# Layer 1's first product in groups of four samples, with two levels of Strassen's method

## The chip, the cores and the metric

The kernel runs on one core of a Trainium2 chip, as one launch. The metric is the time of that launch on the device in microseconds (us), the median of several executions. A profile of one execution shows where the time goes. The engines are named as the profile names them: PE is TensorE (matmuls; PEld is its loading of weights), DVE is VectorE, ACT is ScalarE, POOL is GpSimd, SP is SyncE, which here only issues DMA transfers.

## The reference

Four graph layers work on a batch of 128 samples, each with 128 nodes of 512 features; every layer ends in a residual sum and a layer norm. The change is in layer 1, a hypergraph convolution with a hidden width of 1024:

```
H  = (adj != 0);  w = adj's first row                  # 128 x 128 per sample
Dn = 1 / (H w);   Be = 1 / (column sums of H)          # guarded against 0
conv(x, W, b) = Dn * (H (Be * (H^T (x W^T)))) + b

h = relu(conv(x, W1, b1))       # 512 -> 1024
h = layer_norm(h, gamma, beta)
y = conv(h, W2, b2)             # 1024 -> 512
x = layernorm(x + (y + x))
```

Layer 0 is a graph diffusion with three weight matrices, layer 2 an attention over a product of adjacency and exp(tanh), layer 3 an eight-head attention with the adjacency as mask. All is in fp32.

## The kernel before, in words

**A recorded plan.** The kernel doesn't issue instructions as its Python runs. The names `pe`, `ve`, `ac`, `po` and `sp` are recorders: each call adds an operation with its tiles and with the current `plan.key`, a number that says when the operation should come (one unit is one pair of samples). At the end `Plan.emit` (line 356) orders all operations with a list scheduler that has a cost for each operation and a latency between engines, and issues them. That is why nearly all instructions carry line 367 of `emit`: one tells them apart by engine, operation and tile. Every engine then works through its own queue in that fixed order.

**Tiles.** SBUF tiles have kinds with a fixed number of places: `four` (1024 columns, 12 places, and more that come from other kinds once those are no longer needed), `sq` (pairs of 128x128), `col` (small columns), `out` (layer 0's results), `k` (the small matrices K). The big tile `first` holds layer 0's weights (kind `w7`) at first; later the same space holds layer 1's second weights (`w28`) and layer 3's query and key weights (`q7`). The dictionary `later` says which places come free when which others are done. PSUM has eight banks: six of kind `bank` and two (`t0`, `t1`) that layer 0 uses for itself and that are banks later.

**Strassen's method.** A product of a pair of samples (two blocks of 128 rows) with a weight matrix is done with seven products instead of eight. `strassen` (line 549) issues them in three banks: in bank `al` four products accumulate one after the other, and between two of them the sum so far is read out, so each waits for the eviction before it. `take` is a dictionary of evictions, by name of the result. `operands` makes the four sums of the left side on POOL. With `twice`, the method is used at two levels on two pairs of samples: seven calls of `strassen`, one for each of the outer products, 49 inner products in all, of one matmul each. Outer sums of the left side come from `lefts`, and two additions per half join the outer results. Layer 0's product and layer 3's query and key product use `twice` already.

**Layer 1 before** (`layer1`, called for each of 64 pairs of samples) has eight stages with the keys of `WHEN1`: load x1 and the adjacency; turn it, make H and the scaled H; make K = H Be H^T and Dn; multiply x1 with K (YT) and form `operands`, and also make q, which holds 2 x + b2 and the term of beta; the first product with W1; the turning of h by way of DRAM; the second product with W2; the product with K, layer norm, store. The first product is one-level Strassen with two matmuls of 512 columns in each of the seven products. Each eviction on DVE scales by Dn and adds b1 on its way out of PSUM:

```
return lambda p: ve.scalar_tensor_tensor(d, p, scale[u], b, op0=OP.mult, op1=OP.add)
```

When a quarter of the result is complete, `then` runs relu on ACT on its 512 columns, takes its statistics on DVE, and after a sample's second half normalizes the sample.

**The order of the layers.** The last lines start `layer0`, `layer1` and `layer23` one after the other in keys, with `LAG1` and `LAG2` as distance, so that a layer's first groups overlap with the last of the layer before. `prepare1`, `prepare2`, `prepare_w` and `prepare3` load and combine the weights of later layers while an earlier layer runs.

Of the kernel before, what the change touches and what calls it, by code (L numbers as in the profile page):

```python
# [13 lines left out]
AF = mybir.ActivationFunctionType  # L14
# [3 lines left out]
P = 128  # L18
# [19 lines left out]
WHEN1 = (-3.0, -2.3, -1.25, -.8, 0, 1.0, 1.4, 2.0)  # L38
WHEN2 = (-2.4, -2.0, -1.45, -1.15, -.7, .3, .5, 2)
WHENV, WHENS, WHENP, WHENO = (.9, 1.9), (2.2, 3.2), (3, 4), (3.5, 4.5)  # L40
LAG1, LAG2 = 1, -.25
# [22 lines left out]
SIZE = {"four": U * D, "sq": U * (P + 2), "bank": D, "col": 12, "row": D, "w28": 7168, "q7": 7 * 2 * P,  # L64
# [311 lines left out]
def kernel(  # L376
# [19 lines left out]
    for kind, n, at in (("w7", 7, 0), ("q7", 7, 0), ("w28", 1, 7 * SIZE["q7"])):  # L396
        places[kind] = [first[:, at + k * SIZE[kind]:at + (k + 1) * SIZE[kind]] for k in range(n)]
        if kind != "w7":
            for k in range(n):
                lo, hi = at + k * SIZE[kind], at + (k + 1) * SIZE[kind] - 1  # L400
                later[kind, k] = [("w7", i) for i in range(lo // SIZE["w7"], min(hi // SIZE["w7"], 6) + 1)]
    slots = {"w7": 7, "out": OUTS, "q7": 0, "w28": 0, "sq": SQS, "col": COLS, "row": ROWS, "bank": 6, "t0": 1, "t1": 1,
# [35 lines left out]
    def four():  # L438

        return tile_of("four", U, D)  # L440
# [25 lines left out]
    class Seven:  # L466
# [5 lines left out]
        def __getitem__(self, key):  # L472
            return self.tiles[key[1]][(key[0], *key[2:])]

# [482 lines left out]
    def prepare1():  # L957
# [4 lines left out]
        WT["w1"] = Seven([four().rearrange("p c f -> p c f") for _ in range(7)])  # L962
        yield from load_T(WT["w1"], [w1], 2, D)
        gb = four().rearrange("p u f -> p (u f)")
# [15 lines left out]

    def layer1(i0):
        x1 = load_rows(x1d[i0 // U])
        ab = from_dram(adj[i0:i0 + U], sq)
        yield
        AT = sq()
        turned(AT, ab)
        HT = sq()
        cnt = col(U)
        for b in range(U):
            ve.tensor_scalar(HT[:, b], AT[:, b], 0.0, None, op0=OP.not_equal, op1=OP.add,  # L990
                                    accum_out=cnt[:, b:b + 1])
        po.tensor_scalar(cnt, cnt, 1.0, None, op0=OP.max)
        po.tensor_tensor(cnt, cnt, minus1, OP.pow)
        M = P + 2
        HB = sq(M)
        for b in range(U):
            po.tensor_scalar(HB[:, b, :P], HT[:, b], cnt[:, b:b + 1], None, op0=OP.mult)
        po.tensor_copy(HB[:, :, P:P + 1], AT[:, :, 0:1])
        po.memset(HB[:, :, P + 1:P + 2], 1.0)
        yield  # L1000
        pk = bank()
        with plan.together():
            for b in range(U):
                pe.matmul(pk[:, b * M:(b + 1) * M], HT[:, b], HB[:, b], start=True, stop=True)
        K = tile_of("k", U, M)
        ac.copy(K.rearrange("p b n -> p (b n)"), pk[:, :U * M])
        Dn = col(U)
        dsafe = col(U)
        deg = pk[:, :U * M].rearrange("p (b n) -> p b n", n=M)[:, :, P]
        ve.tensor_scalar(dsafe, deg, 1.2e-38, None, op0=OP.max)  # L1010
        ve.reciprocal(dsafe, dsafe)
        ve.scalar_tensor_tensor(Dn, deg, 0.0, dsafe, op0=OP.is_gt, op1=OP.mult)
        drd = col(U)
        po.tensor_tensor(drd, Dn, K[:, :, P + 1], OP.mult)
        yield
        YT = four().rearrange("p u (c n) -> p u c n", n=P)
        for b in range(U):
            pt = bank()
            with plan.together():
                for c in range(C):  # L1020
                    pe.matmul(pt[:, c * P:(c + 1) * P], x1[:, b, c * P:(c + 1) * P], K[:, b, :P],
                              start=True, stop=True)
            ac.copy(YT[:, b].rearrange("p c n -> p (c n)"), pt)
        ops = operands(*blocks(YT))

        q = four()
        for b in range(U):
            po.tensor_tensor(x1[:, b], x1[:, b], b2h, OP.add)
            ac.mul(q[:, b], bw2, drd[:, b:b + 1])
            ve.scalar_tensor_tensor(q[:, b], x1[:, b], 2.0, q[:, b], op0=OP.mult, op1=OP.add)  # L1030
        yield
        h = [four() for _ in range(U)]
        dn = [Dn[:, b:b + 1] for b in range(U)]
        take = biased_take((h[0][:, 0], h[0][:, 1], h[1][:, 0], h[1][:, 1]),
                           b1_b * 2, dn)
        sts = [col(12) for _ in range(U)]
        left = [2, 2]

        def then(f, b, g):
            def run(p):  # L1040
                t = h[b][:, g]
                f(p)
                ac.activation(t, t, AF.Relu)
                stats(sts[b], g, t)
                left[b] -= 1
                if not left[b]:
                    nmr, rstd = norm_terms(sts[b], 2)
                    ac.activation(h[b], h[b], AF.Identity, bias=nmr, scale=rstd)
            return run

        for k, b, g in (("c11", 0, 0), ("c12", 0, 1), ("c21", 1, 0), ("c22", 1, 1)):
            take[k] = then(take[k], b, g)
        strassen(ops, WT["w1"], 2, D, take)
# [297 lines left out]
```

## Time and profile before

| | before |
|---|---|
| time, median of 3 | 5501.85 us (5497.74 to 5502.41) |
| span in the profile | 5492.0 us |
| instructions | 88697 |
| DMA, mean share of 16 engines | 131 GB/s moved |
| layer 0 | about 0 to 1300 us |
| layer 1 | about 1350 to 3160 us |
| layers 2 and 3 | about 3200 us to the end |

The layers are told apart by the forms of their matmuls: 386 columns in layer 0, 512 and 256 in layer 1, 256 and 128 after it. In the page's timeline each digit is the busy share of a fortieth of the span, in tenths:

```profile
PE   8999999999999999999999999999999999999998
DVE  6787887877676666666666678777777777777776
ACT  2333333334333333333333334444444444444444
POOL 6777777766666666666666578888888888888887
```

DVE and POOL are the least busy in the stretch from the eleventh to the twenty-third digit, which is layer 1.

### The profile page before, as it was taken

The numbers are of one execution on the slowest core, as the hardware profiler recorded it, in microseconds if no ns is written. First come the engines' busy times: TensorE is split into PE (matmuls) and PEld (weight loads), VectorE is DVE, ScalarE is ACT, GpSimd is POOL, SyncE is SP. The second block draws the span as 40 slices with busy tenths as digits, with TensorE's granted clock in tenths as the row PEclk, the third lists the DMA queues.
The fourth block names the chain that finished last, engine by engine and source line by source line (L and its number), as shares of the span: only waits on it lengthen the run. The fifth ranks groups of instructions, "written<-read, shape, count | busy, mean of one in ns | idle before, by whom it ended". The sixth has DMA issues, their size and how long they took to land.

```text
span 5492.0 us, 88697 instructions
## 1 busy us (share of the span) xinstructions
PE 5408.3 (98%) x27801; PEld 4003.2 (73%) x27801; DVE 4015.5 (73%) x9010; ACT 2255.4 (41%) x5839; POOL 3993.5 (73%) x5848
## 2 busy tenths in 40 slices
PE   8999999999999999999999999999999999999998
PEld 4555555554666666666666788989999998999987
DVE  6787887877676666666666678777777777777776
ACT  2333333334333333333333334444444444444444
POOL 6777777766666666666666578888888888888887
PEclk9999999999999999999999999999999999999999
DMA  3333333333444444333444445555555555555543
GB/s 89 111 94 105 93 98 104 95 106 120 134 130 120 120 116 116 114 115 115 120 120 120 132 122 155 166 159 161 162 158 157 164 154 158 166 162 155 160 151 128
DMA packets 752508, 717.39 MB, mean 131 GB/s; under 512 B 261787, under 2 KB 573091, under 8 KB 752038
## 3 DMA queue, kind: packets, MB, share of 16 engines
q1 hardware_dynamic: 750534, 709.11, 43.3%
q8 instruction: 221, 3.62, 0.3%
q10 hardware_dynamic: 1504, 2.62, 0.2%
q14 instruction: 249, 2.04, 0.1%
HBM read 393.76 MB, written 317.72 MB: 130 GB/s over the span
## 4 chain that ended last, share of the span: by engine, by line
PE 87%; DVE 4%; DMA 3%; POOL 2%; issue 2%; ACT 1%; SPq 1%; DVEq 0%; POOLq 0%; ACTq 0%
PE bank L367 66%; PE t L367 20%; DVE out L367 2%; SPq L367 1%; DVE col L367 1%; DMA out<-h 1%; DVE four L367 1%; ACT out L367 1%; POOL col L367 0%; POOL out L367 0%; POOL four L367 0%; DVE first L367 0%; DVE sq L367 0%; DMA four<-in_x_dram 0%; POOL first L367 0%
## 5 line engine op out<-in xcount | busy, mean ns | idle before, releaser
L367 DVE TENSOR_TENSOR out<-bank,out 128x386 f32<-128x386 f32 (+1 forms) x1949 | 951.1, 506 | 524.8 <-PE bank L367 444.0
L367 PE MATMUL bank<-first,four 128*128 128x386 f32 (+3 forms) x4416 | 1292.8, 446 | 25.4 <-DVE out L367 10.1
L367 PEld LDWEIGHTS bank<-first,four 128*128 128x128 f32 (+2 forms) x4416 | 744.5, 189 | 550.8 <-DVE out L367 129.2
L367 PE MATMUL bank<-four,out 128*128 128x256 f32 (+2 forms) x2100 | 707.7, 474 | 0.3 <-DVE four L367 0.2
L367 POOL TENSOR_TENSOR out<-out 128x256 f32<-128x256 f32 (+3 forms) x424 | 492.8, 1173 | 253.3 <-DVE out L367 202.7
L367 PEld LDWEIGHTS bank<-four,out 128*128 128x128 f32 (+1 forms) x2100 | 375.9, 190 | 253.4 <-issue 208.3
L367 ACT COPY out<-bank 128x258 f32<-128x258 f32 (+2 forms) x581 | 243.3, 421 | 627.9 <-PE bank L367 495.1
L367 PE MATMUL bank<-first,out 128*128 128x256 f32 (+3 forms) x2168 | 469.2, 372 | 1.6 <-DVE out L367 1.1
L367 POOL TENSOR_SCALAR col<-col 128x1 f32<-128x1 f32 (+1 forms) x704 | 174.5, 251 | 383.6 <-DVE col L367 357.9
L367 PEld LDWEIGHTS bank<-first,out 128*128 128x128 f32 (+2 forms) x2168 | 387.1, 188 | 56.2 <-DVE out L367 3.0
L367 POOL TENSOR_TENSOR col<-col,neghalf 128x1 f32<-128x1 f32 x640 | 392.7, 617 | 18.3
L367 ACT ACTIVATE out<-out,col,col 128x512 f32<-128x512 f32 (+1 forms) x260 | 231.8, 898 | 394.3 <-POOL col L367 385.3
L367 ACT ACTIVATE four<-four,col,col 128x512 f32<-128x512 f32 (+1 forms) x294 | 268.6, 922 | 281.6 <-POOL col L367 250.3
L367 DVE TENSOR_TENSOR four<-bank,four 128x256 f32<-128x256 f32 x573 | 236.2, 418 | 176.6 <-PE bank L367 167.0
L367 PE MATMUL bank<-out,first 128*128 128x128 f32 (+3 forms) x2192 | 344.9, 298 | 1.8 <-DVE out L367 0.7
L367 PE MATMUL bank<-four,first 128*128 128x128 f32 (+3 forms) x1612 | 317.3, 331 | 1.8 <-DVE out L367 1.5
L367 PEld LDWEIGHTS bank<-out,first 128*128 128x128 f32 (+2 forms) x2192 | 290.2, 186 | 27.6 <-issue 3.1
L367 POOL TENSOR_TENSOR four<-four,four 128x256 f32<-128x256 f32 (+2 forms) x369 | 305.1, 830 | 6.0 <-PE bank L367 1.1
L367 DVE BATCH_NORM_STATS2 col<-four 128x6 f32<-128x512 f32 x370 | 252.4, 684 | 49.9 <-ACT four L367 48.0
L367 PE MATMUL bank<-first 128*128 128x128 f32 (+1 forms) x2036 | 285.5, 278 | 3.1 <-DVE out L367 1.9
L367 PEld LDWEIGHTS bank<-first 128*128 128x128 f32 (+1 forms) x2036 | 257.5, 188 | 17.6 <-DVE out L367 2.6
L367 PEld LDWEIGHTS bank<-four,first 128*128 128x128 f32 (+2 forms) x1612 | 246.5, 189 | 28.4 <-issue 2.3
(431 smaller groups left out, 12130.4 us busy)
## 6 DMA issues: line engine op xcount, KB each, us to landing
out<-h SPq DMA_DIRECT2D x96, 512.0 KB, 4.4
h<-four SPq DMA_DIRECT2D x304, 128.0 KB, 2.4
four<-in_x_dram SPq DMA_DIRECT2D x512, 64.0 KB, 2.0
four<-in_x_dram SPq DMA_DIRECT2D x62, 512.0 KB, 3.8
x1d<-four SPq DMA_DIRECT2D x62, 512.0 KB, 2.8
out<-S SPq DMA_DIRECT2D x54, 512.0 KB, 4.3
h<-out SPq DMA_DIRECT2D x208, 128.0 KB, 2.4
S<-out SPq DMA_DIRECT2D x49, 512.0 KB, 3.1
```

The lines of the kernel that those rows point to most:

```text
L367: call(*map(real, args), **{n: real(a) for n, a in kw.items()})
```

## The change

Layer 1 now works on groups of four samples (two pairs, index r), as layer 0 and layers 2 and 3 do. Its first product goes through `lefts` and `twice`. The bias and the scale differ by column and by row, and inside the two-level scheme a partial result belongs to several outputs, so they can't be added in the eviction any more: the evictions become plain (ACT copies and DVE adds), and scale, bias and relu follow as operations on the whole row of 1024 columns.

```
 def prepare1():
-        WT["w1"] = Seven([four().rearrange("p c f -> p c f") for _ in range(7)])
+        WT["w1"] = Seven([four() for _ in range(7)])
         yield from load_T(WT["w1"], [w1], 2, D)
+        for k, j in enumerate((B11, B21, T2, T1, B22, T3, N4)):
+            yield
+            WT["w1"].tiles[j] = Split(WT["w1"].tiles[j], tile_of("q3", 3, 2 * P))
+            combine(WT["w1"].tiles[j], (ve, po)[k % 2])
...
 def layer1(i0):
...
-        take = biased_take((h[0][:, 0], h[0][:, 1], h[1][:, 0], h[1][:, 1]),
-                           b1_b * 2, dn)
...
-        strassen(ops, WT["w1"], 2, D, take)
...
+        left = lefts(YTs)
+        yield
+        base = plan.key
+
+        h = [[tile_of("h" if i0 + 2 * U < B else "four", U, D) for _ in range(U)] for _ in range(2)]
+        twice(left, WT["w1"], 2 * P,
+              lambda r, half: [h[r][b][:, half, m * 2 * P:(m + 1) * 2 * P] for b in range(U) for m in range(2)],
+              lambda r, half: [h[r][b][:, half] for b in range(U)], [lambda d: plain_take(*d)] * 2, STEP1)
+        loads = []
+        for r, i in enumerate(both):
+            plan.key = base + STEP1 * (5, 7)[r]
+            for b in range(U):
+                t = h[r][b].rearrange("p g f -> p (g f)")
+                ve.scalar_tensor_tensor(t, t, dns[r][b], rows1[:, :2].rearrange("p g f -> p (g f)"),
+                                        op0=OP.mult, op1=OP.add)
                 ac.activation(t, t, AF.Relu)
+                sts = col(12)
+                for g in range(2):
+                    stats(sts, g, h[r][b][:, g])
+                nmr, rstd = norm_terms(sts, 2)
+                ac.activation(t, t, AF.Identity, bias=nmr, scale=rstd)
```

Around it:

- The second-level parts of W1 (new kind `q3`) and the tiles of h (new kind `h`, seven places) lie in the space of layer 0's weights. The query and key weights of layer 3 (`q7`) now wait for `q3` and `h` to be done, so `prepare2` moves from the first half of layer 1 to its end, and `prepare_w` and `prepare3` move later too.
- x1 and K aren't kept in SBUF through a group: K is stored to DRAM and loaded again, and x1 is loaded a second time, before the last stage. q is made there.
- The keys of layer 1's stages are new (`WHEN1`, `STEP1` = 0.22 for the step between the seven outer products, `WHENH`, `WHENW`, `WHENG`), and `LAG2`, the distance to layers 2 and 3, goes from -0.25 to 1.5.

## The prediction

> **What bounds the kernel now.** I read the engines' shares first, then the chain that ended last, then the busy time by stage, and last the order of time inside one stage.
>
> ```profile
> PE 5408.3 (98%) x27801; PEld 4003.2 (73%) x27801; DVE 4015.5 (73%) x9010; ACT 2255.4 (41%) x5839; POOL 3993.5 (73%) x5848
> PE 87%; DVE 4%; DMA 3%; POOL 2%; issue 2%; ACT 1%; SPq 1%; DVEq 0%; POOLq 0%; ACTq 0%
> ```
>
> TensorE is busy 98% of the span and holds 87% of the chain. Four windows follow: the passage from layer 0 to layer 1, the middle of layer 1, the passage to layers 2 and 3, and these two layers.
>
> ```profile
> 1235.70:1373.00 137.30, 124.34 (x408) 64.94 (x407) 109.10 (x248) 58.03 (x125) 83.01 (x127) 0.99 0.40 120
> 1700.00:2980.80 1280.80, 1278.38 (x4929) 863.94 (x4929) 781.03 (x1544) 481.57 (x775) 788.02 (x1322) 1.00 0.40 117
> 3157.90:3295.20 137.30, 130.10 (x864) 115.84 (x863) 105.03 (x244) 53.01 (x167) 100.02 (x135) 0.99 0.41 122
> 3295.20:5354.70 2059.50, 2051.72 (x15200) 1864.77 (x15199) 1622.72 (x3882) 947.83 (x3212) 1729.44 (x2423) 1.00 0.52 159
> ```
>
> The columns after the length are PE, PEld, DVE, ACT, POOL. In layer 1 PE is busy 99.8%, DVE 61%, POOL 62%. In layers 2 and 3 PE stays at 99.6% with DVE at 79% and POOL at 84%: that is how full the helpers may be without PE noticing. The two passages lose 13.0 and 7.2 us. So time comes only from less PE work, as long as the other engines keep up.
>
> Now the order of time on PE, start and length first:
>
> ```profile
> 2000.12 3.60 PE L367 MATMUL bank<-four,out 128*128 128x512 f32 x8
> 2003.55 1.88 PE L367 MATMUL bank<-out,out 128*128 128x512 f32 x4
> 2012.21 1.89 PE L367 MATMUL t<-first,four 128*128 128x256 f32 x8
> 2013.94 1.89 PE L367 MATMUL bank<-first,four 128*128 128x256 f32 x8
> ```
>
> Each matmul leaves two records (layer 1 has 54 matmuls a pair of samples, 108 records; 4929 records are 45.6 pairs, 28.05 us each). From start to start, eight records of 512 columns take 3.43 us, so one matmul takes 857 ns; eight of 256 take 1.73 us, so one takes 432 ns.
>
> Last, the engines that share work around it:
>
> ```profile
> 2011.79 2.02 DVE L367 SCALAR_TENSOR_TENSOR out<-four,out 128x512 f32<-128x512 f32 x2
> 2011.39 1.27 POOL L367 TENSOR_TENSOR four<-four,rows 128x512 f32<-128x512 f32 x1
> 2012.62 1.02 POOL L367 TENSOR_TENSOR col<-col,neghalf 128x1 f32<-128x1 f32 x1
> 2014.54 0.55 POOL L367 TENSOR_TENSOR col<-col,neghalf 128x1 f32<-128x1 f32 x1
> ```
>
> Two DVE operations with two SBUF tensors take 2.02 us beside a POOL operation, and the small POOL operation after it takes 1.02 instead of 0.55 us.
>
> Prices by form, over the whole span (the number before the last bar is the mean of one in ns):
>
> ```profile
> L367 DVE TENSOR_TENSOR four<-bank,four 128x256 f32<-128x256 f32 x573 | 236.2, 418 | 176.6 <-PE bank L367 167.0 <-POOL four L367 2.4 <-issue 0.4
> L367 DVE TENSOR_TENSOR first<-first 128x256 f32<-128x256 f32 x16 | 8.1, 539 | 0.0
> L367 DVE TENSOR_TENSOR four<-four,four 128x1024 f32<-128x1024 f32 x6 | 7.3, 1216 | 0.0
> L367 POOL TENSOR_TENSOR four<-four,four 128x256 f32<-128x256 f32 x202 | 147.6, 731 | 4.1 <-PE bank L367 0.5
> L367 POOL TENSOR_TENSOR four<-four,four 128x512 f32<-128x512 f32 x101 | 128.3, 1272 | 0.8 <-PE bank L367 0.7
> L367 POOL TENSOR_TENSOR four<-four,four 128x128 f32<-128x128 f32 x66 | 30.1, 456 | 1.2
> ```
>
> [...] the first of the two STTs seems to wait until the POOL add ends at 2012.66, and POOL then gives time back. [...] The row of six above agrees (1216 ns); no row has 1024 columns and a scalar, and I take the same. [...] So I price PE by starts, and these agree that PE is full.
>
> **The change, part by part.** Counts are from the two built programs.
>
> 1. *The product itself.* Per four samples, 28 matmuls of 512 columns (7 products, 2 accumulations, 2 pairs) become 49 of 256. In all 896 x 0.857 = 768 us go and 1568 x 0.432 = 677 us come: **PE -91 us**, 2.84 us a group of four. The group's 56.1 us becomes 53.3 us of PE work. Weight loads rise with the matmuls, but one is 190 ns beside 432 ns and stays under it, as in the second product today.
>
> 2. *VectorE.* A group has 2 x 781.03/45.6 = 34.2 us today. It loses 14 evictions with scale (722 to 743 ns, -10.3 us) and gains 41 evictions of 256 columns (418 ns by the row, 380 ns by starts where three stand together): +15.6 to 17.1 us. It also gains four scale-and-bias operations of 1024 columns on two SBUF tensors: 1.22 us each alone, up to 2.1 if they double as the 512-column pair does (1.0 each): +4.9 to 8.4 us. Sum 44.4 to 49.4, or 83 to 93% of 53.3. I take 47. The eviction is also a wait: four products accumulate in one bank in turn, and each waits until the one before is read, so an eviction behind a 1.2 us transpose on VectorE's queue delays PE unless other products are ready. The second product (24 us a group) is such filler.
>
> 3. *GpSimd.* Today 2 x 788.02/45.6 = 34.5 us a group. Added are eight adds of 512 (four for sums of inputs, four that join the partial results; 1.272 us), four more of 256 (0.73) and four of 128 (0.456): 10.2 + 2.9 + 1.8 = +14.9 us. That is 49.4 us, 93% of 53.3. [...] 4 x 1.22 = 4.9 us if each stops an add, 4 x 0.47 = 1.9 if each meets a small operation as in the lines above. So 51.3 to 54.3 us, **96 to 102% of PE's work**; I take 52. This is the narrow place. Behind GpSimd's queue stand the sums that the next products read, so a late GpSimd stops PE.
>
> 4. *ScalarE.* Relu on 1024 columns, once a sample instead of twice on 512, and eight more copies of 256 (372 ns): about 21.1 + 2 = 23 us a group, hidden under PE.
>
> 5. *DMA.* 64 stores and 64 reloads of K (133 KB), 64 second loads of x1 (512 KB): about 50 MB on 717 MB, with the DMA share at 0.40 in layer 1. Hidden.
>
> 6. *Passage into layer 1.* The first weights get their second level: 16 VectorE subtractions (539 ns) and 12 on GpSimd (0.73 us), 8.6 and 8.8 us, beside layer 0's last products. The results lie where layer 0's weights were, so they can't be made earlier. Then the first group has 21 us of short products and no second product as filler, with 17 us of evictions. From 13 us lost I expect 23: +10.
>
> 7. *Passage out.* The query and key weights now need the space of h and of the second-level parts, so their load, turning and combining come after layer 1's last first product instead of beside layer 1. The combining alone is 16 x 0.54 + 4 x 2.33 = 18 us of VectorE. Layer 1's last second products (24 us of PE) and layer 2's first products stand beside it; the later start of layer 2 makes that room. From 7 us lost I expect 15: +8.
>
> Sum for PE's idle time inside layer 1: at 93 to 98% GpSimd I expect 1.5% of a group lost, 0.8 us, 26 us in 32 groups. Bounds: 0.2 us (as full as layers 2 and 3) and 3 us. Total: -91 + 26 + 10 + 8 = -47, **5455 us**.
>
> **The rivals.**
>
> *A (0.50), the forecast:* most of PE's saving stays, some is lost on a nearly full GpSimd. 5455.
>
> *B (0.27), all hidden:* [...] the adds fit in the gaps, the passages cost half: -91 + 6 + 9 = -76, 5426. For it: PE at 99.6% in layers 2 and 3 with the same two-level scheme. Against it: GpSimd is at 84% there, not at 93% or more.
>
> *C (0.13)[...]:* a group takes the 54.3 us of item 3 and about 1 us that its order can't fill, 55.3: -26 + 18 = -8, 5494. For it: POOL's waits on VectorE's statistics are 360 us in the layer 1 window, and a chain of three small operations leaves gaps of 0.1 us. Against it: those waits are mostly slack today.
>
> *D (0.10), slower:* GpSimd full and VectorE at 93% wait for each other, so PE's products arrive late in both: 56.5 us a group, +13, with the passages' 18: 5533. For it: each new VectorE operation waits for a GpSimd add and then stops one. Against it: they are four a group, and the products have six to eight banks.
>
> **How the numbers follow.** A is the likeliest, so the time is 5455. A and B are faster. C spreads over the border: 0.05 faster, 0.08 the same. D is slower. So faster 0.82, same 0.08, slower 0.10. For the range I take B's lower side (nothing lost in layer 1, passages +3: 5415) and C's upper side (5510); D is left out and little else.
>
> **What would show it.** Right: in the middle of layer 1, PE starts of 432 ns in the first product, POOL at 9 tenths, DVE at 8, PE at 97 to 99%, a group at about 54 us; PE waits on POOL's four and out tiles, which it hardly has today; the new 1024-column operation at 1.2 to 2.1 us. Wrong: PE below 96% in layer 1 (C or D), or a passage that loses more than 30 us; a POOL share under 88% would mean I priced its adds too high, and B would be the case.

## The result, and the profile after

The changed kernel takes 5531.85 us (5523.80 to 5539.37), beside 5502.13 us for the kernel before on the same chip: a ratio of 1.0055, 95% interval 1.0038 to 1.0073. It is slower by 30 us (0.55%) where 47 us less were forecast, and outside the range. The page of the changed kernel, engines' shares and then the chain that ended last:

```profile
PE 5368.3 (97%) x29145; PEld 4254.2 (77%) x29145; DVE 4386.7 (79%) x10018; ACT 2317.8 (42%) x5967; POOL 4585.9 (83%) x6372
...
PE 76%; POOL 7%; DVE 6%; DMA 5%; issue 3%; ACT 2%; SPq 1%; POOLq 0%; DVEq 0%; ACTq 0%
```

TensorE's share of the chain fell from 87 to 76%; POOL and DVE carry 13% of it where they had 6, and DMA 5 where it had 3. The busy tenths show where POOL is full:

```profile
PE   8999999999899999999999899999999999999998
...
DVE  6787888877888888888788877777777777877776
...
POOL 6777777767899999999999778888888888888886
```

The stretch of nines on POOL is layer 1. The two eights within PE's row are the passages into and out of it. By windows (start and end, length, then PE, PEld, DVE, ACT, POOL, clock, DMA share, GB/s): passage in, layer 1, passage out, layers 2 and 3.

```profile
1235.70:1520.00 284.30, 251.54 (x1026) 175.51 (x1026) 227.82 (x512) 108.98 (x209) 217.58 (x307) 0.96 0.42 122
1520.00:3040.00 1520.00, 1492.51 (x7144) 1255.73 (x7143) 1246.22 (x2743) 628.23 (x1052) 1450.99 (x2051) 1.00 0.50 149
3040.00:3316.00 276.00, 246.71 (x1376) 211.31 (x1375) 227.94 (x474) 106.09 (x261) 208.53 (x271) 0.96 0.49 151
3316.00:5389.00 2073.00, 2054.93 (x15162) 1853.98 (x15161) 1621.29 (x3869) 949.52 (x3207) 1731.55 (x2410) 1.00 0.51 157
```

In layer 1 POOL is at 95%, DVE at 82%, PE at 98.2% (before 99.8). The passages are idle for 33 and 29 us.

PE's busy share hides small losses: the profile gives eight records of 512 columns 3.60 us, and the next starts after 3.43 (the prediction's lines at 2000.12 and 2003.55). So I took starts: for every matmul record, the time to the next start, less 0.8333 ns a column and 2.6 ns, a line through what records take from start to start in the trace of the kernel before (medians: 216 ns at 256 columns, 324 at 386, 429 at 512). What is left over is loss. The levels mean little (layers 2 and 3 are priced too high by it, hence the minus), the differences between kernels do. The table holds the part that goes with a lower clock too; the expectations below mostly leave it out (0 to 9 us). "Order 3" is the changed kernel with another of its planner's orders, explained below.

| loss in us | before | after | after, order 3 |
|---|---|---|---|
| first 150 us | 37.8 | 42.6 | 36.2 |
| rest of layer 0 | 27.1 | 26.0 | 24.7 |
| passage into layer 1 (280 us) | 21.1 | 49.3 | 40.2 |
| middle of layer 1 | 7.7 | 48.0 | 47.8 |
| passage out (240 us) | 12.4 | 42.8 | 45.4 |
| layers 2 and 3 | -129.9 | -110.6 | -121.4 |
| last 110 us | 0.8 | 4.7 | 2.0 |
| work priced by columns | 5501.5 | 5412.6 | 5409.9 |

The work fell by 89 us (good to about 3: the same kernel is priced at 5412.6 and 5409.9 in its two orders). The losses rose by 126: 40 in the middle of layer 1, 28 and 30 in the passages, 19 in layers 2 and 3, 8 elsewhere, in rounded numbers. The sum, +37, is the difference of the two profiled spans (5528.7 and 5492.0).

One of layer 1's small waits, first on PE, then on DVE (start, length, what, idle time before and its releaser):

```profile
2205.35 0.59 PE L369 MATMUL bank<-four,out 128*128 128x256 f32 x2
2207.27 1.99 PE L369 MATMUL bank<-first,four 128*128 128x256 f32 x8 [1.32 <-DVE out L369]
```

```profile
2205.66 1.25 DVE L369 STREAM_TRANSPOSE four<-out 128x1024 f32<-128x1024 f32 x1 [1.78 <-DMA out<-h]
2206.83 0.38 DVE L369 TENSOR_TENSOR out<-bank,out 128x256 f32<-128x256 f32 x1
```

The matmul needs a bank. DVE reads that bank at 2206.83, behind a transpose of 1.25 us, which itself had kept DVE's queue waiting 1.78 us for a reload of h. This is the case that the prediction's item 2 named; the filler that it counted on didn't stand at that place of PE's fixed queue. Of 27.2 us of PE waits over 60 ns between 1540 and 2980 us, 18.2 end like this, in a read of a bank by VectorE, and 14.8 stand behind a wait for a reload of h (the VectorE operation that released PE, or the one before it, had itself waited for one). VectorE's waits for these reloads in that window (who for whom: us, times, longest), the changed kernel and then the kernel before:

```profile
DVE four L369 <- DMA out<-h: 26.3, 17, 4.8
DVE out L369 <- DMA out<-h: 24.3, 15, 4.0
DVE out L369 <- DMA four<-h: 22.0, 9, 4.4
DVE four L369 <- DMA four<-h: 10.9, 6, 2.7
```

```profile
DVE out L367 <- DMA out<-h: 4.9, 9, 0.9
DVE out L367 <- DMA four<-h: 1.4, 2, 1.0
DVE four L367 <- DMA out<-h: 0.7, 1, 0.7
```

That is 84 us where it was 7. A reload takes 4.8 to 5.0 us from issue to landing in the median, 4.4 before, so the transfer itself is only a little longer. How much of the 84 us comes from that, and how much from when it is issued and where the fixed order puts the transposition, no experiment below singles out.

### The profile page after: what moved, and what is told of

Its sections match the earlier page's. It is cut to its first block, busy times and chain, and to the rows that moved or that the text cites. A ratio compares the mean times of both kernels' runs of the same rounds, so it can differ in the third digit from the quotient of the medians.

```text
span 5528.7 us, 93993 instructions
## 1 busy us (share of the span) xinstructions
PE 5368.3 (97%) x29145; PEld 4254.2 (77%) x29145; DVE 4386.7 (79%) x10018; ACT 2317.8 (42%) x5967; POOL 4585.9 (83%) x6372
## 4 chain that ended last, share of the span: by engine, by line
PE 76%; POOL 7%; DVE 6%; DMA 5%; issue 3%; ACT 2%; SPq 1%; POOLq 0%; DVEq 0%; ACTq 0%
PE bank L369 58%; PE t L369 18%; POOL out L369 2%; POOL four L369 2%; DVE first L369 2%; DVE out L369 2%; POOL col L369 1%; DVE col L369 1%; POOL first L369 1%; DMA out<-h 1%; SPq L369 1%; DVE four L369 1%; DMA four<-in_x_dram 1%; DMA four<-h 1%; DVE sq L369 1%
## 5 line engine op out<-in xcount | busy, mean ns | idle before, releaser
L369 PE MATMUL bank<-first,four 128*128 128x386 f32 (+3 forms) x4804 | 1464.8, 449 | 40.9 <-DVE out L369 23.1
L369 PEld LDWEIGHTS bank<-first,four 128*128 128x128 f32 (+2 forms) x4804 | 852.8, 189 | 601.1 <-DVE out L369 138.0
L369 DVE TENSOR_TENSOR first<-bank,first 128x256 f32<-128x256 f32 x1351 | 546.3, 415 | 141.7 <-PE bank L369 122.9
L369 PE MATMUL bank<-first,out 128*128 128x256 f32 (+3 forms) x2414 | 560.7, 372 | 15.0 <-DVE first L369 8.5
L369 PE MATMUL bank<-four,out 128*128 128x256 f32 (+2 forms) x1568 | 381.0, 367 | 1.2 <-DVE first L369 0.8
L369 POOL TENSOR_TENSOR first<-first 128x512 f32<-128x512 f32 (+3 forms) x264 | 302.4, 1161 | 77.1 <-DVE first L369 56.1
L369 ACT ACTIVATE four<-four,col,col 128x512 f32<-128x512 f32 x262 | 211.0, 812 | 312.4 <-POOL col L369 279.0
L369 PE MATMUL bank<-four,four 128*128 128x256 f32 (+2 forms) x1156 | 291.8, 371 | 13.2 <-DVE first L369 11.9
L369 POOL TENSOR_TENSOR four<-four 128x256 f32<-128x256 f32 (+2 forms) x375 | 275.1, 746 | 35.3 <-DVE four L369 27.9
L369 PEld LDWEIGHTS bank<-four,out 128*128 128x128 f32 (+2 forms) x1568 | 263.9, 188 | 40.4 <-issue 3.2
```

Of the source, the lines that this page charges most:

```text
L369: call(*map(real, args), **{n: real(a) for n, a in kw.items()})
```

## The experiments

18 kernels ran besides the two. Times are compared by their ratio to the kernel before on the same chip (whose median lay between 5494.5 and 5500.4). "Loss" is the measure of the table.

**1. The order.** The planner makes three orders, each of the last two with due times from the one before, and keeps the one that its own prices call shortest. Of the kernel before it keeps the third (ends by its prices 5558.0, 5438.8, 5424.3), of the changed kernel the second (5502.5, 5377.6, 5398.0). These are its estimates, not times.

*second_order*: the changed kernel keeps the last order.

```diff
-            if other[2] < end:
-                start, place, end = other
+            start, place, end = other
```

> The changed kernel keeps the last of the three orders that its planner makes instead of the one that the planner prices best; in the kernel before it is the last that is kept, in the changed one the second. If layers 2 and 3 lose 18 us because of that order, these layers get 10 to 20 us faster here. Layer 1 and its passages get another order too, by the planner's price about 20 us worse in all. If the order isn't the cause, layers 2 and 3 keep their PE rate of 7.31 records per us (7.39 before).

*before_one_round*: the kernel before keeps its second order.

```diff
-    plan.emit(places)
+    plan.emit(places, 1)
```

> The kernel before with the second of its planner's three orders instead of the third. If the order explains the loss in layers 2 and 3, this kernel loses 10 to 20 us there and is at 5510 to 5525 us. If not, layers 2 and 3 keep their 7.39 records per us and the time is within 8 us of 5502.

Measured: second_order 5500.29 us, ratio 1.0005 (0.9997 to 1.0014); before_one_round 5532.38, 1.0059 (1.0042 to 1.0076), above both of its forecasts. So the order that the planner rates 20 us worse is 31 us better on the chip (28 by the ratios). At equal rank the two kernels are level: 5500 and 5499 in the third order, 5532 and 5532 in the second. The 30 us of the result go with the order that was kept; the 89 us of saved work vanish in either. In layer 1 the loss is the same 48 us in both orders, but not the same waits: in the third only 2.0 of 21.7 us of PE's waits stand behind a reload of h.

**2. Less load in the order that stands.** Here operations become short only when issued, the planner still prices them whole, and the order is that of the changed kernel.

*portfree*: the four scale-and-bias operations of a group read one SBUF tensor instead of two; b1 is left out. Two cases were set against each other: that the second SBUF tensor of these operations costs layer 1 its saving, by what they and GpSimd's operations take from each other, or that GpSimd's own load does.

```diff
-                ve.scalar_tensor_tensor(t, t, dns[r][b], rows1[:, :2].rearrange("p g f -> p (g f)"),
-                                        op0=OP.mult, op1=OP.add)
+                plan.add(DVE, lambda o, i, s, bias, **kw: nc.vector.tensor_scalar(
+                    o, i, s, None, op0=OP.mult, op1=OP.add, accum_out=junk.real()[:, :1]), "scalar_tensor_tensor",
+                    (t, t, dns[r][b], rows1[:, :2].rearrange("p g f -> p (g f)")), {})
```

> The changed kernel in its own order; only the four scale-and-bias operations a group (1024 columns, two SBUF inputs) are replaced by a VectorE operation of about the same length with one SBUF input (b1 is left out of the sum). [...] PE's lost time in the middle of layer 1 (48 us of 1520 in the changed kernel, 11 of 1700 before) falls to 10 to 20 us and the kernel to about 5495 to 5505. If GpSimd's own load is the cause, layer 1 changes by less than 10 us and the time is 5522 to 5535. Passages and layers 2 and 3 stay as they are in both cases.

*joins8*: GpSimd's additions that join the outer products take 8 columns.

```diff
-                    po.tensor_tensor(d, v, y, OP.add)
+                    if narrow:
+                        plan.add(POOL, lambda d, v, y, op: nc.gpsimd.tensor_tensor(d[:, :8], v[:, :8], y[:, :8], op),
+                                 "tensor_tensor", (d, v, y, OP.add), {})
...
```

> The changed kernel in its own order; the four additions a group on GpSimd that join outer results in layer 1 work on 8 columns instead of 512 (the rest of these columns is left out of the sum). GpSimd gets about 4 us a group lighter[...]. If GpSimd's load[...] is the cause, PE's lost time in the middle of layer 1 falls from 48 to below 20 us, the kernel to 5495 to 5505. If only the exclusion of the four new VectorE operations matters, it falls by less than 10 us and the time stays over 5520.

*both_light*: joins8, and the scale-and-bias operation on 8 columns, without b1.

```diff
-                ve.scalar_tensor_tensor(t, t, dns[r][b], rows1[:, :2].rearrange("p g f -> p (g f)"),
-                                        op0=OP.mult, op1=OP.add)
+                plan.add(DVE, lambda o, i, s, bias, **kw: nc.vector.tensor_scalar(o[:, :8], i[:, :8], s, None, op0=OP.mult),
+                         "scalar_tensor_tensor", (t, t, dns[r][b], rows1[:, :2].rearrange("p g f -> p (g f)")), {})
```

> The changed kernel in its own order of work; in layer 1 GpSimd's join additions and VectorE's scale-and-bias operations each take 8 columns of their tile only, and the bias b1 is left out, so that both helpers are light at once; the output then lacks most of the join sums. Theory A (layer 1's small waits are the helpers' load, GpSimd's and VectorE's together: each alone gave 8 or 9 us because the other took over as the narrow one): the 48 us lost in the middle of layer 1 fall to 20 or less and the time to 5485 to 5505. Rival B (the waits come from the order in which the planner puts the products and their inputs, not from load): the lost time stays at 35 or more and the time at 5515 or more.

*light_passages*: in the preparation of the weights, W1's second-level sums, the products and row sums for W2 and the sums of the query and key weights take 8 columns; the first-level sums of W1 and W2 stay whole.

```diff
-            combine(W[j])
+            combine(W[j], small=True)
...
-            ve.tensor_tensor(st, st, gb, OP.mult)
+            few_ve(st, st, gb, OP.mult)
```

> The changed kernel in its own order of work; the second-level sums of W1, the products and row sums that prepare W2 and the sums of the query and key weights take 8 columns only, so most of those sums are left out. Theory A (the passages into and out of layer 1 lose time because the preparation of the new weights loads VectorE and GpSimd while TensorE needs them): the passages' loss of 49 and 43 us falls to 25 or less each and the time to 5480 to 5500. Rival B (the passages wait for transfers or for buffers to come free): each stays within 8 us of what it was and the time at 5520 or more.

*drain8*: VectorE's additions out of the first product's banks take 8 columns; ScalarE's copies stay whole.

```diff
+    def drained(d, p, b, op):
+        if plan.narrow:
+            plan.add(DVE, lambda d, p, b, op: nc.vector.tensor_tensor(d[:, :8], p[:, :8], b[:, :8], op),
+                     "tensor_tensor", (d, p, b, op), {})
+        else:
+            ve.tensor_tensor(d, p, b, op)
...
-                return lambda p: ve.tensor_tensor(d, p, b, OP.add)
+                return lambda p: drained(d, p, b, OP.add)
```

> The changed kernel in its own order of work; VectorE's additions that read layer 1's first product out of its PSUM banks take 8 of 256 columns, so most of those sums are left out. Theory A (TensorE's small waits in layer 1 are for banks: a product is now half as long, and its bank's next product waits until VectorE has read it): the 48 us lost in the middle of layer 1 fall to 25 or less, and the time to 5495 to 5510. Rival B (the waits are for operands from GpSimd and ScalarE, the banks being read in time): 40 us or more stay, and the time is 5515 or more.

| | ratio to before | loss, layer 1 | passage in | passage out |
|---|---|---|---|---|
| after | 1.0055 | 48.0 | 49.3 | 42.8 |
| portfree | 1.0044 (1.0029 to 1.0059) | 39.7 | 49.3 | 42.5 |
| joins8 | 1.0034 (1.0022 to 1.0046) | 38.7 | 42.1 | 40.8 |
| both_light | 1.0024 (1.0014 to 1.0034) | 45.9 | 39.7 | 40.1 |
| light_passages | 1.0025 (1.0017 to 1.0033) | 43.9 | 36.3 | 37.5 |
| drain8 | 1.0036 (1.0021 to 1.0050) | 33.9 | 44.2 | 44.5 |

By the medians every one gains a little, but only both_light and light_passages lie clear of the changed kernel's interval (1.0038 to 1.0073), and none gains what its main theory asked for. The losses are of one execution each: the one of joins8 was 15 us faster than that kernel's median, that of light_passages 8 us faster, that of both_light 10 us slower, so a difference of a few us in this table means little. light_passages takes 13 us from the passage in and 5 from the passage out, so the preparation's load is at most a part of the first and little of the second. portfree is the plainest trial of what the second SBUF tensor costs, since order and work are otherwise the same: GpSimd's operations get shorter, as shown below, and its share of layer 1 falls from 95 to 90%, yet PE loses only 8 us less; 14.7 us of its waits still stand behind a reload of h. both_light looked like the end of the load theory, and I formed another: short products turn the banks round too fast for VectorE. drain8 half agreed (14 us). Both readings left out that the order itself was made for the full load.

**3. The same load, in the third order.** All work is done in these.

*third_early* starts W2's preparation 3.5 units earlier. The same edit also moves W1's second-level sums earlier, by half a unit to 3.5.

```diff
         for k, j in enumerate((B11, B21, T2, T1, B22, T3, N4)):
-            yield
             WT["w1"].tiles[j] = Split(WT["w1"].tiles[j], tile_of("q3", 3, 2 * P))
```

> The planner's third order kept, and the preparation of W2 begins 3.5 units of the key work earlier than in the changed kernel; all work is done. Theory A (W2's preparation comes too late for its first readers in layer 1, which is where VectorE's two waits of 17 and 9 us came from): the loss in the passage into layer 1 falls by 15 us or more, and the time is 5475 to 5490. Rival B (the preparation only moves the same load to an earlier stretch, which is as full): 5495 to 5505, as the third order alone gave 5500.

*third_b2ve* moves the addition of b2 from GpSimd to VectorE; *before_b2ve* does so in the kernel before; *third_b2ve_priced* also tells the planner that the scale-and-bias operation is 350 ns longer.

```diff
-                po.tensor_tensor(x1[:, b], x1[:, b], b2h, OP.add)
+                ve.tensor_tensor(x1[:, b], x1[:, b], b2h, OP.add)
```

> The planner's third order kept, and the 128 additions of the second bias to the residual move from GpSimd to VectorE in layer 1; all work is done. Theory A (GpSimd's load is what leaves TensorE the small waits in layer 1, and VectorE has room): the 48 us lost in the middle of layer 1 fall to 25 or less and the time to 5465 to 5480, faster than both kernels. Rival B (VectorE[...] becomes as narrow): 5495 to 5510.

> The kernel before, with the second bias added by VectorE in place of GpSimd as in the fastest version so far; all work is done. If that edit helps only where GpSimd is nearly full, as after the change, the kernel before stays within 4 us of its time, 5496 to 5504. If it is worth as much here as after the change, about 7 us, the change itself still brings nothing: 5493 or less.

> The third order and the bias additions on VectorE as before, and the planner's price of VectorE's scale-and-bias operation raised by 350 ns, from 1.2 to the 1.6 to 1.9 us that it takes beside GpSimd, so that the order leaves time behind it; all work is done. Theory A (late drains behind this operation cause the waits, as the planner takes it for shorter than it is): the layer-1 loss of 59 us falls to 45 or less and the time to 5475 to 5487. Rival B (the price only spreads the same waits): 5490 to 5500.

*third_x1q* takes that addition out of layer 1 altogether: layer 0's last stage makes it on GpSimd and stores the sum beside x1.

```diff
+            for b in range(U):
+                po.tensor_tensor(x0[:, b], x0[:, b], b2h, OP.add)
+            sp.dma_start(x1q[i // U], x0)
...
-            x1 = load_rows(x1d[i // U])
+            x1 = load_rows(x1q[i // U])
...
-                po.tensor_tensor(x1[:, b], x1[:, b], b2h, OP.add)
```

> The planner's third order kept, and the second bias is added to the residual in layer 0's last stage, where GpSimd has room, and stored beside it, so that neither helper does it in layer 1; 16.8 MB more are written to memory; all work is done. Theory A (layer 1's helpers are the limit; less work for them there is time): layer 1 loses 35 us or less and the time is 5470 to 5488, under the version with these additions on VectorE. Rival B (the order of drains decides, and load does not): 5490 to 5505.

*third_x1q_early* joins it with third_early; *before_x1q* is the same edit in the kernel before.

> The fastest version so far with W2's preparation 3.5 units of the key work earlier; all work is done. Theory A (with GpSimd relieved the passage into layer 1 has room for it): the passage loses 35 us or less, against 49, and the time is 5460 to 5472. Rival B (the earlier start made the third order 13 us slower before, and does the same here): 5480 to 5490.

> The kernel before, with the second bias added to the residual in layer 0 and stored beside it, as in the fastest version so far; all work is done. If the edit is worth time only because the change fills the helpers, the kernel before stays within 0.1% or gets slower by the added transfers: 5494 to 5505. If it is worth as much here, 5480 or less, and the change itself still brings nothing.

| | us | ratio to before | loss, layer 1 |
|---|---|---|---|
| third_early | 5513.17 | 1.0023 (1.0015 to 1.0031) | 54.8 |
| third_b2ve | 5493.27 | 0.9988 (0.9981 to 0.9994) | 60.1 |
| third_b2ve_priced | 5510.52 | 1.0030 (1.0017 to 1.0043) | 66.0 |
| before_b2ve | 5498.71 | 1.0006 (0.9999 to 1.0013) | 11.5 |
| third_x1q | 5475.21 | 0.9968 (0.9956 to 0.9980) | 29.5 |
| third_x1q_early | 5476.61 | 0.9965 (0.9952 to 0.9978) | 27.7 |
| before_x1q | 5564.70 | 1.0126 (1.0109 to 1.0143) | 46.8 |

third_early fails both of its theories: the passage in loses 50 us, against 40 in the third order. The time is 10 us worse than that of the third order by the ratios, and third_x1q_early is level with third_x1q and outside both of its forecasts: this edit brings nothing. Whether W2's earlier start alone would, it doesn't tell. Moving the addition to VectorE (third_b2ve) makes layer 1 worse (60 us lost against 48); the whole is a little faster, by a passage out of 30 us instead of 45 and layers 2 and 3 by 9. third_b2ve_priced, which should have cured that by a truer price, is 23 us slower than third_b2ve by the ratios and loses 66 us in layer 1, so its theory fails. Taking the addition out of layer 1 gives 20 us by the ratios, and third_x1q, with all work done, beats both kernels. before_x1q meets neither of its forecasts and doesn't compare cleanly: the kernel before used x1 from its product for the residual too, so it now needs a second load and one more buffer in each group, and loses 69 us. The other edit, before_b2ve, is worth nothing there.

**4. Less load, planned anew.** Now the short operations are recorded short, so the planner makes its order for them; the third order is kept in all.

*light_replanned* is both_light in this way.

```diff
-                    po.tensor_tensor(d, v, y, OP.add)
+                    po.tensor_tensor(d[:, :8], v[:, :8], y[:, :8], OP.add)
...
-                ve.scalar_tensor_tensor(t, t, dns[r][b], rows1[:, :2].rearrange("p g f -> p (g f)"),
-                                        op0=OP.mult, op1=OP.add)
+                ve.tensor_scalar(t[:, :8], t[:, :8], dns[r][b], None, op0=OP.mult)
```

> GpSimd's join additions and VectorE's scale-and-bias operations of layer 1 take 8 columns, without b1, so most join sums are left out; unlike in the run with both light, the planner is told the shorter operations and makes its order for them, and its third order is kept. Theory A (the helpers' load costs the time, and an order made for the full load keeps the products apart even where the load is gone): layer 1 loses 20 us or less, against 43 with the old order, and the time is 5440 to 5465. Rival B (the turn-round of the PSUM banks costs it whatever the load): 35 us or more stay, and the time is 5480 or more.

*drain_replanned* is drain8 in this way.

> VectorE's additions out of the banks of layer 1's first product take 8 columns, so most of those sums are left out; the planner is told so, and its third order is kept. Theory A (turn-round of banks: a short read lets the bank's next product start sooner, and the order can use that): layer 1 loses 20 us or less and the time is 5450 to 5475. Rival B (the load of GpSimd[...] costs it, and VectorE's reads are not the limit): 30 us or more stay, and the time is 5480 to 5500.

*scale_replanned* and *joins_replanned* are the second and the first half of light_replanned. Theory A of both is that the sum of GpSimd's time and that of VectorE's operations on two SBUF tensors sets the loss; rival B, that GpSimd's time alone does.

> VectorE's scale-and-bias operations of layer 1 take 8 columns, without b1; the join additions on GpSimd stay whole; the planner makes its order for that, and its third order is kept. Theory A ([...] in layer 1 the two together claim 113% of the time in the changed kernel): taking away VectorE's largest claim brings it to about 100%, layer 1 loses 35 us or less, against 48, and the time is 5465 to 5485. Rival B (GpSimd's own work is the narrow place[...]): 45 us or more stay, 5493 or more.

> The other half: GpSimd's join additions of layer 1 take 8 columns, so most join sums are left out; the scale-and-bias operations stay whole; the planner makes its order for that, and its third order is kept. Theory A[...]: the claims fall to about 104%, layer 1 loses 35 us or less and the time is 5465 to 5485. Rival B (GpSimd's own work): nearly the whole gain of the run with both light and planned anew, 5450 to 5462.

The last two columns are of the window 1540 to 2980 us: GpSimd's share of busy time, and "claims", GpSimd's time plus that of VectorE's operations on two SBUF tensors. It can pass 100%: two engines' times are added, and time in which an operation is held up counts as busy (the scale-and-bias operation takes 1586 ns in the mean in the changed kernel, 1229 at the shortest). In the last two rows 3 of the per cent are the 8-column operation that takes the place of scale and bias; it reads one SBUF tensor.

| order 3 of | us | ratio to before | loss, layer 1 | GpSimd | claims |
|---|---|---|---|---|---|
| the changed kernel | 5500.29 | 1.0005 | 47.8 | 96% | 112% |
| drain_replanned | 5502.89 | 1.0008 (1.0002 to 1.0015) | 63.8 | 94% | 113% |
| third_b2ve | 5493.27 | 0.9988 | 60.1 | 87% | 111% |
| third_x1q | 5475.21 | 0.9968 | 29.5 | 87% | 104% |
| joins_replanned | 5477.75 | 0.9962 (0.9948 to 0.9976) | 32.1 | 87% | 104% |
| scale_replanned | 5476.32 | 0.9961 (0.9946 to 0.9976) | 39.5 | 90% | 100% |
| light_replanned | 5451.94 | 0.9919 (0.9904 to 0.9933) | 27.9 | 83% | 92% |

The windows of drain_replanned and of light_replanned (same columns as above):

```profile
1540.00:2980.00 1440.00, 1409.58 (x6684) 1178.16 (x6683) 929.73 (x2569) 591.85 (x982) 1354.07 (x1914) 1.00 0.49 146
```

```profile
1540.00:2980.00 1440.00, 1427.92 (x6850) 1192.98 (x6849) 1033.04 (x2634) 599.03 (x1010) 1198.29 (x1968) 1.00 0.50 152
```

In drain_replanned VectorE is down to 930 us of 1440, 65%, less than in light_replanned, and still PE waits for it; what is nearly full there is GpSimd, at 94%. The waits of PE there (who for whom: us, times, longest):

```profile
PE bank L369 <- DVE first L369: 16.4, 31, 1.6
PE t L369 <- DVE first L369: 5.7, 17, 0.6
```

They are put down to VectorE's reads of banks, as in the changed kernel, while a third of VectorE's time is free: the last releaser need not be the engine that is short of time. That GpSimd's fullness made VectorE late here isn't read from these lines; of PE's 30 us of waits in this window 6.6 stand behind a reload of h.

What goes with the two groups of the third order is the claims: 111 to 113% with 48 to 66 us lost in layer 1 (third_b2ve_priced, at 112%, is the 66), 104% and less with 28 to 40; in layers 2 and 3, where PE is 99.6% busy in the kernel before, they are 90%. Within a group they order nothing: scale_replanned, with fewer claims than joins_replanned, loses more. In the order made for the full load they tell nothing: both_light has claims of 91% and loses 46, drain8 115% and loses 34. third_b2ve suggests that it is not GpSimd's share alone: that fell to 87% as in third_x1q, but the claims stay at 111%, since VectorE's addition reads two SBUF tensors too. There is a rival to that reading which no run excludes: VectorE is 85% busy in third_b2ve, more than in any of the others of this table, and may be late by its own load.

The durations show directly that these operations hold each other up. Groups by form in the same window (count, then busy us and mean ns of one), the changed kernel and then scale_replanned:

```profile
L369 DVE SCALAR_TENSOR_TENSOR first<-first,col,rows 128x1024 f32<-128x1024 f32 x104 | 164.8, 1586 | 0.8
L369 POOL TENSOR_TENSOR first<-first 128x512 f32<-128x512 f32 x106 | 154.4, 1469 | 22.2 <-DVE first L369 19.6 <-PE t L369 1.5 <-DMA sq<-in_adj_dram 0.9
L369 POOL TENSOR_SCALAR sq<-sq,col 128x128 f32<-128x128 f32 x106 | 87.2, 833 | 0.1
```

```profile
L368 POOL TENSOR_TENSOR first<-first 128x512 f32<-128x512 f32 x105 | 133.4, 1274 | 81.9 <-DVE first L368 81.9
L368 POOL TENSOR_SCALAR sq<-sq,col 128x128 f32<-128x128 f32 x106 | 70.2, 672 | 0.1
```

Between these two the order differs as well. portfree keeps the changed kernel's order, and shows the same:

```profile
L369 POOL TENSOR_TENSOR first<-first 128x512 f32<-128x512 f32 x107 | 135.2, 1273 | 29.7 <-DVE first L369 29.4
L369 POOL TENSOR_SCALAR sq<-sq,col 128x128 f32<-128x128 f32 x106 | 67.8, 650 | 0.1
```

With one SBUF tensor instead of two in VectorE's operation, GpSimd's untouched additions fall from 1469 to 1273 ns, and its scaling of H from 833 to 650. In the kernel before that scaling takes 620 ns. Single operations in the changed kernel's trace show how, in the same window. Of the 104 scale-and-bias operations 39 began within a GpSimd addition of 512 columns, and each of them ended 1.08 to 1.13 us after that addition's end. The other way round, 34 such additions that began within a scale-and-bias operation ended 1.13 to 1.14 us after its end. The shortest of these operations take 1.23 and 1.25 us in all, so the later one did most of its work after the earlier one's end: in these traces they exclude each other, in both directions. One of each kind (start and length; POOL's line is two additions, the first of them 2.25 us long, until 1614.18):

```profile
1611.77 1.28 DVE L369 SCALAR_TENSOR_TENSOR first<-first,col,rows 128x1024 f32<-128x1024 f32 x1
1611.93 4.47 POOL L369 TENSOR_TENSOR first<-first 128x512 f32<-128x512 f32 x2 [0.63 <-DVE first L369]
1613.30 1.97 DVE L369 SCALAR_TENSOR_TENSOR first<-first,col,rows 128x1024 f32<-128x1024 f32 x1
```

A caution: a plan made anew is another order, and two orders of one kernel differ by 31 us. One run of this kind with 24 us proves little. By the ratios three that bring the claims to 104% or less each gain 20 to 24 us over the third order, both halves together gain 47, and the four that leave the claims at 111% or more (with third_early) go from 9 us gained to 14 lost. Nor is the whole gain in layer 1: of light_replanned's 48 us by the spans 20 are in its middle and 22 in the passages (32 and 31 us against 40 and 45), and scale_replanned's layer 1 loses 39.5 us, as portfree's does in the old order, and not the 35 or less that its theory asked for; light_replanned's 27.9 misses its 20 or less too. So it is shown that lighter helpers with a plan made for them are worth this time in all; that what GpSimd and VectorE's operations on two SBUF tensors take from each other is what limits layer 1 is the likeliest reading, not a proof.

## Why the prediction was wrong

*Item 1, -91 us:* right; the priced work fell by 89.

*Item 3, "the narrow place":* right in kind and share. GpSimd is busy 52.4 us a group (95% of 54.9) where 52 were taken, and it and VectorE's new operation cost each other time: 1586 ns for the new operation, between the bounds of 1.22 and 2.1 us, and 1469 ns for GpSimd's addition of 512 columns, which takes 1273 in portfree. But the waits that it should have shown, of PE on GpSimd's tiles, are 2.4 of 27 us there.

*The idle time inside layer 1, "0.8 us, 26 us in 32 groups":* mis-sized. It is 40 us more than before in the 1520 us of the middle, 1.5 us a group, between its bounds of 0.2 and 3. Item 2 had named the late read of a bank and then let the second product fill it; rival D had "six to eight banks" set against it. Neither held: 18 of PE's 27 us of waits end in a late read of a bank. What made VectorE late is shown in part only: 15 us stand behind reloads of h, and VectorE and GpSimd lengthen each other's operations (the 1586 and 1469 ns of item 3).

*Item 5, DMA "hidden":* the bandwidth was right (a DMA share of 0.50), but the reloads of h are on PE's path, as these 15 us show. The item priced what the new transfers move, and not when h comes back.

*Items 6 and 7, "+10" and "+8":* these failed most. The passages cost 28 and 30 us more. Item 6 counted the weights' preparation, which by light_passages is about 13 us of the passage in and 5 of that out, in one execution. The fill of layer 1 was taken for a part of 10; in the profile one wait alone is as long (start, length, idle time before):

```profile
1411.78 1.22 PE L369 MATMUL bank<-four,four 128*128 128x256 f32 x2 [11.34 <-DVE first L369]
```

In the third order a like wait is for GpSimd's scaled H of layer 1's start:

```profile
1399.70 1.38 PE L368 MATMUL bank<-sq,sq 128*128 128x130 f32 x4 [11.65 <-POOL sq L368]
```

A group of four samples has a longer chain of small steps before its first product than a pair has. That this is the rest of the passages is argued, not shown: their cause stays open beyond the preparation. Of the 58 us, an estimated 13 go with a lower clock, the 0.96 of the two windows (from the 16 us of the last section, less 3 that the kernel before has by the same estimate: 6.8 us of half clock there, 6.4 of them busy).

*The sum had no term for layers 2 and 3*, whose code is untouched. They take 19 us more. In the third order 11 of these go, and with the other stages 31 in all. That the planner would keep an order that is worse on the chip was nowhere in the working; it treated the order as given.

By spans the forecast was -47 and the profiles show +37. The difference of 84 is 2 in the product, 14 in layer 1, 41 in the passages, 19 in layers 2 and 3, and 8 at the ends and in layer 0. *Rival D* gave nearly the measured time, 5533, by luck: it came to it by 56.5 us a group in layer 1; a group took 54.9 (7144 records in 1520 us, 258 a group). Its cause, GpSimd and VectorE both full in layer 1, was not there: VectorE stood at 82%. *Rival C*'s bound, GpSimd with what VectorE's new operations take from it, at 55.3 us a group, is closest to what the runs showed in layer 1. That its 5494 is near to the third order's 5500 is luck too: it has 18 us for the passages, which lose 52 more in that order. Of the forecast's own signs, those for layer 1 came out right (PE 98%, POOL at 9 tenths, DVE at 8, a group at 54.9 us); a passage that loses more than 30 us, its sign of being wrong, came true twice by starts (49 and 43 us).

## What to carry to other kernels

Fewer matmul columns were worth here what the helpers could follow (89 us of work saved, no time gained at equal rank of the order): before changing the product, add GpSimd's time to that of VectorE's operations on two SBUF tensors. Where the sum passed 110% here, taking work off both (into layer 0, where GpSimd was at 6 to 7 tenths) brought 20 us, and moving it from one to the other made the stage worse. Look also at what the late engine's queue had waited for before: for half of PE's waits in layer 1 of the changed kernel, by time, that was a reload from DRAM. When a planner sets the order, a change is always the change and a new order: compare orders of equal rank before blaming or praising the code, and when an operation is made light for a test, plan anew, or the old order keeps much of the wait. A wait put down to one engine says who came last, not who was short of time: in drain_replanned it named VectorE with a third of its time free.

## What the runs showed of the hardware

A VectorE operation that reads two SBUF tensors and a GpSimd operation hold each other up, and this reaches small and large GpSimd operations alike: in one and the same order a GpSimd addition of 512 columns goes from 1273 to 1469 ns and a scaling of 128 columns from 650 to 833 ns in the mean when four VectorE operations of 1024 columns in each 55 us read two SBUF tensors and not one; these take 1586 ns, where the operation of the same width on one tensor took 1267. And in the two passages, where TensorE is idle for 33 us of 284 and 29 of 276, its granted clock is 0.96 on average, against 1.00 in the full layers. By the profile's record of the clock it was at half for 24 us of the one and 20 us of the other, in stretches of 3.4 to 17 us. Records of 256 columns start 427 ns apart in the median in these stretches, 216 in the middle of layer 1; TensorE was busy for 12 and 20 us of them, and half of that, 16 us, is an estimate of their part in the 92 us lost there.
